# Two graph layers on one core: waits of a per-node stage as listed rounds, the first bias additions as a tied GpSimd step, and the last strip's square and copy on VectorE

## The chip, the cores and the metric

One core of a Trainium2 chip runs the whole program. A core has five engines with a queue each: TensorE (PE, matmuls; its weight loads are shown apart as PEld), VectorE (DVE), ScalarE (ACT), GpSimd (POOL) and SyncE (SP, which here only issues DMAs). An engine starts the instructions of its queue in order, so an instruction that waits holds up everything behind it on that engine. The metric is the device time of one execution in microseconds (us), the median of several runs; lower is better.

## The reference

Inputs are `x` of 3327 x 64 (fp32), and a symmetric 0/1 matrix `adj` of 3327 x 3327. Two graph layers follow each other, each with a layer norm and a ReLU ahead of it and a residual after it.

```
h  = relu(layernorm(x));     x = x + L0(h, adj)      # hyperbolic attention
h  = relu(layernorm(x));     out = x + L1(h, adj)    # decaying sum over neighbours
L0: adj_att[i,j] = sigmoid(left[i] + right[j] + b) * adj[i,j]
    support[i]   = sum_j adj_att[i,j] * logmap(h[i], h[j])        # N x N x 64
    L0 = proj(expmap(h, support))                                 # per node
L1: rank = cumsum(adj, axis=1); w[i,j] = adj[i,j] * 0.5^(neighbours of i at or behind j), at most 100 neighbours
    L1 = w @ (h @ weight) + bias
```

The sums over j in L0 and L1 are the heavy part; `expmap`, `proj`, the residual and the second layer norm are work per node, that is on 3327 x 64 numbers or less.

## The kernel before, in words

**Tiling.** Nodes are padded to 26 blocks of 128 (`NB`). The columns i are cut into four strips (`STRIPS`): blocks 0 to 7, 8 to 15, 16 to 21 and 22 to 25; they are called strips 0 to 3 here. Within a strip the loop at L1276 runs over rounds, one source block j at a time (two in strip 3, since it is half as wide). Strips 0, 1 and 2 have 26 rounds each and strip 3 has 13, so n counts rounds 0 to 90: 26 to 51 are strip 1, 52 to 77 strip 2, 78 to 90 strip 3.

**One round.** ScalarE computes the two `gelu` passes over the logmap's inner products (L881, on the PSUM tile `pq`), the sigmoid's tanh (L671) and sometimes the reading of the neighbour counts `pc` out of PSUM into bytes (`read`, L656). VectorE does `pair_one` (L676: tanh times adjacency, both operands in SBUF), often `read` (L658 or L660), `edges` (L622: the 0/1 mask of a later round) and `pair_two` (L681: times `pq`, which is in PSUM). TensorE does the counts (L633, L634), the inner products (L688, L689) and the sum over j (L701). The counts are what layer 1 later turns into its weights.

**Per-node stage.** When a strip's sum over j is ready, `strip_out` copies it out of PSUM (L1205, L1207), `turn` transposes it, and `post` (L1021) runs the per-node work: dot products, `expmap`, `proj`, residual, layer norm, and at last `s2`, the half-precision pair of rows that the matmuls of layer 1 take as weights. `post` is a Python generator that runs while the program is being written, and sets where its instructions stand between those of the rounds. For strips 0 to 2 (`hidden`) its small arithmetic is on GpSimd and it is spread over the rounds of the next strip. A `yield` of `BIG`, `LATER`, `ACT` or `POOL` hands the turn back: `advance` (L1236) takes portions up to a limit and stops at a `LATER`; a step that asks for `ACT` or `POOL` is emitted at the next place of a round where `asked_of` (L1246) allows it. In strips 0 to 2 each round calls `advance` once, and in strip 3 twice. `after(time)` (L1075) emits the GpSimd arithmetic asked for so far and then yields `LATER` so many times:

```
yield from [LATER] * math.ceil(time / ROUND[k + 1])
```

with `ROUND` a round's length per strip. The three waits are `after(7)` before the tanh (L1136), `after(16)` before the four wide GpSimd steps (L1172 to L1175), and `after(6)` before the normalized rows (L1193). This gives 2, 5, 2 rounds for strip 0, 3, 6, 3 for strip 1, and 4, 9, 4 half rounds for strip 2. What has not been emitted when the next strip's stage begins is emitted at once by `finish` (L1253). Such a stage keeps its tiles (`w`, `u`, `agg` and others) in single buffers, so the next strip's stage reuses them.

**A tie.** TensorE, VectorE and ScalarE keep the order in which the program is written. GpSimd's order is arranged by a planner from the data each instruction needs. A wide GpSimd step is therefore tied to a place: `on_pool` (L1085) first writes one element of the result out of the newest mask (L1089), which makes the step wait for that mask.

**The end.** After round 90 the bytes of 22 of the 26 source blocks are decoded into weights, either by one ScalarE instruction (L1376) or by two on VectorE (L1379, L1380), while TensorE runs through the blocks j of `order` (L1394), seven matmuls of L1269 each. Decoding runs `LEAD` blocks ahead of them. Of the 22 decodings the 3rd, 5th, 8th, 10th, 13th, 15th, 18th and 20th are on ScalarE. In the same loop the rest of strip 2's stage and all of strip 3's stage (not hidden: its arithmetic is on VectorE, powers apart) are advanced. The last four blocks, 22 to 25, need strip 3's `s2`; their matmuls (from L1438) come after that, interleaved with copying out of PSUM (L1417 to L1421), the matmul with `weight` (L1429), the last addition (L1431) and the stores (L1434, L1436). The layer's `bias` is added to the residual `x_sb` before that: blocks 0 to 15 by four GpSimd instructions written in the loop over `order` and tied to nothing, the rest by VectorE in the closing part (both L1392).

Of the kernel before, what the change touches and what calls it, by code (L numbers as in the profile page):

```python
# [12 lines left out]
F32 = mybir.dt.float32  # L13
# [5 lines left out]
AF = mybir.ActivationFunctionType  # L19
ALU = mybir.AluOpType  # L20
# [3 lines left out]
P = 128  # L24
N = 3327
NB = 26
NP = NB * P
D = 64
K = D + 2
STRIPS = [(0, 8), (8, 8), (16, 6), (22, 4)]  # L30
# [6 lines left out]


PORTIONS, LAST = (2, 4, 4, 8), 8
BIG, LATER, ACT, POOL = 4, 99, 100, 101  # L40
ROUND = (3.5, 3.5, 2.8, 1.9)

LEAD = 7
BESIDE, GAPS = (1, 2, 3, 4), (2, 4)
ACT_DECODES = (2, 5)

GSTRIPS = [(0, 7), (7, 7), (14, 6), (20, 6)]
GFMAX = 7 * P
# [400 lines left out]
def fast(ctx, tc, x, adj_t, r, w_att, b_att, weight, bias, out, flag):  # L449

    nc = tc.nc
    V, A, G, T = nc.vector, nc.scalar, nc.gpsimd, nc.tensor
    const = ctx.enter_context(tc.tile_pool(name="f_const", bufs=1))
# [7 lines left out]
    def across(src, n, name):  # L461
        t = const.tile([P, n], F32, name=name)
        nc.gpsimd.dma_start(t, bass.AP(tensor=src.tensor, offset=src.offset, ap=[[0, P], [1, n]]))
        return t
# [61 lines left out]
    def wide(t, n):  # L526
        return t[:, :, None].to_broadcast([P, n, D])
# [11 lines left out]
    s2 = const.tile([P, NB, 2, D], F16, name="s2")  # L539
# [122 lines left out]
    wide_step, last_on_act, last_mask = [False], [False], [None]  # L662
# [202 lines left out]
    for to, of in ((jz[:D], iz[D:]), (jz[D:], iz[:D]), (ju[:D], iu[:D]), (ju[D : D + 3], iu[D + 3 : D + 6]),  # L865
                   (ju[D + 3 : D + 6], iu[D : D + 3]), (ju[KB : KB + 7], iu[D:])):
        nc.gpsimd.dma_start(to[:, first_i], of)
    bias_b = across(bias, D, "bias_b")
    for half in (slice(0, D), slice(D, P)):
        nc.gpsimd.dma_start(w2[half], weight)  # L870

# [149 lines left out]
    def post(agg, k):  # L1021
# [5 lines left out]
        b0, nb = STRIPS[k]  # L1027
        bs = slice(b0, b0 + nb)
        hidden = k + 1 < len(STRIPS)
        asked_of_w = []  # L1030
        W = Asked(G if hidden else V, asked_of_w)

        def tile_of(name, *dims):
            return pool.tile([P, *dims], F32, name=name if hidden else name + "_last")

        def mul(y, a, b):
            W.tensor_mul(y, a, b)
# [32 lines left out]
        def do_asked():  # L1070
            for do, args, kwargs in asked_of_w:
                do(*args, **kwargs)
            asked_of_w.clear()

        def after(time):  # L1075

            for do, args, kwargs in asked_of_w:
                do(*args, **kwargs)
                if not hidden:
                    yield from [LATER] * 2 if kwargs.get("op") == ALU.pow else [1]  # L1080
            asked_of_w.clear()
            if hidden:
                yield from [LATER] * math.ceil(time / ROUND[k + 1])

        def on_pool(op, to, *of):  # L1085
            if hidden:
                yield POOL
                if last_mask[0] is not None:
                    G.tensor_copy(to[:, 0, :1], last_mask[0][:, :1])  # L1089
                getattr(G, op)(to, *of)  # L1090
                yield 0
            else:
                getattr(V, op)(to, *of)  # L1093
                yield BIG
# [4 lines left out]
        hs, v, xs = hw[:, bs, :D], agg[:, :, :D], x_sb[:, bs]  # L1099
# [3 lines left out]
        t0, t1, k_, y2, rn, rt = (tile_of(n, nb) for n in ("t0", "t1", "k", "y2", "rn", "rt"))  # L1103
        u, w = tile_of("u", nb, D), tile_of("w", nb, D)
# [26 lines left out]
        root(rn, t0)  # L1131
        mul(t0, t0, rn)
        mul(t0, t0, sk[:, bs])
        yield from after(7)
        yield ACT
        A.activation(k_, t0, AF.Tanh)  # L1136
        yield 0
# [30 lines left out]
        W.tensor_scalar(rn, rn, maxnorm, 1.0, op0=ALU.mult, op1=ALU.min)  # L1168
        mul(of_end, of_end, both(rn))
        mul(of_end[:, 0], of_end[:, 0], ih[:, bs])  # L1170
        yield from after(16)
        yield from on_pool("tensor_mul", w, hs, wide(of_end[:, 0], nb))  # L1172
        yield from on_pool("tensor_mul", u, v, wide(of_end[:, 1], nb))
        yield from on_pool("tensor_add", v, xs, w)
# [3 lines left out]

        V.tensor_reduce(t0, xs, AX.X, ALU.add)
        yield BIG  # L1180
        W.tensor_scalar(t0, t0, 1.0 / D, None, op0=ALU.mult)
        do_asked()
        yield from on_pool("tensor_sub", w, xs, wide(t0, nb))
        yield ACT
        A.activation(u, w, AF.Square)
        yield 0
        V.tensor_reduce(t0, u, AX.X, ALU.add)
        yield BIG
        W.tensor_scalar(t0, t0, 1.0 / D, EPS_LN, op0=ALU.mult, op1=ALU.add)
        root(rn, t0)  # L1190
        W.tensor_scalar(rn, rn, HS, None, op0=ALU.mult)
        yield from after(6)
        V.scalar_tensor_tensor(w, w, 0.0, wide(rn, nb), op0=ALU.max, op1=ALU.mult)  # L1193
        yield BIG
        yield ACT
        A.copy(s2[:, bs, 0], w)
        yield 0
        yield from on_pool("tensor_sub", s2[:, bs, 1], w, s2[:, bs, 0])

    def strip_out(k):  # L1200
# [58 lines left out]
    late = STRIPS[-1][0]  # L1259
# [16 lines left out]
    for n in range(2, R):  # L1276
        k, lo, hi = rounds[n]
        m, w = n + AHEAD, span(n)
# [84 lines left out]
    with tc.tile_pool(name="l1", bufs=2, reuse_waits="tile") as l1, tc.manual_schedule(engines=IN_ORDER):  # L1363
        decoded = 0

        def decode(j):

            nonlocal decoded
            if j in JD:
                return behind(j)  # L1370
            spare = decoded % (7 + len(JD)) - 7
            wt = weight_of[:, spare] if spare >= 0 else l1.tile([P, NP], U16, name="wt", bufs=7)
            decoded += 1
            to = by_parity(wt)
            if decoded * ACT_DECODES[0] % ACT_DECODES[1] < ACT_DECODES[0]:
                A.activation(to, behind(j).rearrange("p (k r) -> p r k", r=2), AF.Copy, scale=128.0)  # L1376
            else:
                pairs_of = behind(j).bitcast(U16)
                V.tensor_scalar(to[:, 0], pairs_of, 0xFF, 7, op0=ALU.bitwise_and, op1=ALU.logical_shift_left)  # L1379
                V.tensor_scalar(to[:, 1], pairs_of, 0xFF00, 1, op0=ALU.bitwise_and, op1=ALU.logical_shift_right)  # L1380
            return wt

        every = [*order, *range(late, NB)]
        weights = {j: decode(j) for j in every[: len(JD) + 1]}
        stages.append(Stage(per_node(len(STRIPS) - 1, pa)))
        pw[6] = ps.tile([P, FMAX], F32, name="pc")
        for n, j in beside:
            add(j, behind(j), n)

        def bias(b0, nb, engine=G):  # L1390
            xb = x_sb[:, b0 : b0 + nb]
            engine.tensor_add(xb, xb, bias_b[:, None, :].to_broadcast([P, nb, D]))  # L1392

        for i, j in enumerate(order):  # L1394
            for jn in every[: i + 1 + LEAD]:
                if jn not in weights:
                    weights[jn] = decode(jn)
            list(asked_of(ACT))
            list(asked_of(POOL))
            advance(LAST)  # L1400
            for n in range(len(chunks)):
                if j not in JD or n > 4:
                    add(j, weights[j], n)
            if i % 4 == 3 and i < STRIPS[-2][0]:
                bias(i - 3, 4)
        finish()
        for j in range(late, NB):
            if j not in weights:
                weights[j] = decode(j)
        kept_of = [l1.tile([P, min(NP - 1024 * q, 1024)], F32, name="ow" if q < 3 else "ow_last", bufs=2 if q < 3 else 1)  # L1410
                   for q in range(4)]

        def copied(n):
            q, r = chunks[n]
            to = kept_of[q].rearrange("p (k r) -> p r k", r=2)
            if r is None:
                V.tensor_copy(to, by_parity(pw[n][:, :256]))  # L1417
            elif r == 0:
                V.tensor_copy(to[:, 0], pw[n])
            else:  # L1420
                A.copy(to[:, 1], pw[n])  # L1421

        def close(q):
            for h in range(0, 8 if q < 3 else 2, 4):
                b0 = 8 * q + h
                nb = min(4, NB - b0)
                pc = pw[2 * q + h // 4]
                for b in range(nb):
                    T.matmul(pc[:, b * D : (b + 1) * D], kept_of[q][:, (h + b) * P : (h + b + 1) * P], w2s, start=True, stop=True)  # L1429
                o = l1.tile([P, 4, D], F32, name="o", bufs=4)  # L1430
                V.tensor_add(o[:, :nb], pc[:, : nb * D].rearrange("p (b d) -> p b d", d=D), x_sb[:, b0 : b0 + nb])  # L1431
                full = nb if b0 + nb < NB else nb - 1
                f0 = b0 * P
                nc.sync.dma_start(out[f0 : f0 + full * P, :].rearrange("(b p) d -> p b d", p=P), o[:, :full])  # L1434
                if full < nb:
                    nc.scalar.dma_start(out[f0 + full * P : N, :], o[: N - f0 - full * P, full])  # L1436

        for n in range(len(chunks)):  # L1438
            for j in range(late, NB):
                add(j, weights[j], n)  # L1440
            copied(n)
            if n == 2:
                bias(STRIPS[-2][0], late - STRIPS[-2][0], V)
                bias(late, NB - late, V)
            if n > 0 and n % 2 == 0:
                close(n // 2 - 1)
        close(3)
# [52 lines left out]
```

## Time and profile before

| | |
|---|---|
| median of 3 runs | 398.67 us (398.03 to 398.76) |
| the profiled execution, its own time | 398.52 us |
| its span, first to last instruction | 396.7 us |
| busy: DVE, PE, ACT, POOL | 364.2, 350.1, 348.5, 143.2 us |
| DVE, PE, ACT busy from 217 to 290 us (73 us, strip 2) | 71.89, 69.76, 71.84 us |
| DVE, PE, ACT busy from 345 to 377 us (32 us, decoding) | 29.39, 30.12, 22.56 us |
| from the last store's issue (389.2 us) to the end of the span | about 7.5 us |

The busy times say that no single engine is the limit over the whole span: three engines are each near nine tenths. Which of them ends last has to be read stretch by stretch. Rounds of strip 2 take about 2.7 us and of strip 3 about 3.7 us. In a line of the timeline the first number is the start, the second the duration, then engine, source line, operation and tiles; what stands in brackets is how long the engine sat idle before it, and what it waited for.

### The profile page before, as it was taken

To read this page: it belongs to the slowest core of one execution; us is meant where nothing else is said; L and a number is where in the kernel's file an instruction comes from. 1 tells how busy PE (TensorE), PEld (TensorE's weight loads), DVE (VectorE), ACT (ScalarE), POOL (GpSimd) and SP (SyncE) were. 2 spreads that over 40 slices of the span, in tenths; PEclk is the share of its full clock that TensorE was granted. 3 is DMA by queue.
4 is the path that set the end of the run, shared out by engine and by line. 5 is a ranking of instruction groups with operands and counts; after the bars stand their busy time and mean duration, and the time that the engine had idled before them with its cause. 6 is when DMAs were issued, how large, how long until landed. Compare 5 with 4: busy or idle time off the path is not lost.

```text
span 396.7 us, 4776 instructions
## 1 busy us (share of the span) xinstructions
PE 350.1 (88%) x1460; PEld 149.3 (38%) x1460; DVE 364.2 (92%) x551; ACT 348.5 (88%) x401; POOL 143.2 (36%) x279
## 2 busy tenths in 40 slices
PE   0067999999999899999998999999977899999892
PEld 0053333333333333333333354444433333344362
DVE  3999999999999999999999999999998999798941
ACT  2589999999999999999999999999988899697510
POOL 8136200000000166932133674851248678234100
PEclk9999999999999999999999999999999999999996
DMA  7314555455557455545445445555644430000022
GB/s 208 150 43 132 177 141 145 142 161 156 159 159 211 133 154 158 159 127 164 137 129 151 121 134 161 153 136 151 192 133 135 122 107 0 2 0 1 2 47 48
DMA packets 23299, 49.00 MB, mean 124 GB/s; under 512 B 8789, under 2 KB 9245, under 8 KB 23265
## 3 DMA queue, kind: packets, MB, share of 16 engines
q1 hardware_dynamic: 20993, 47.66, 41.2%
q10 hardware_dynamic: 1808, 0.46, 0.6%
q0 software_dynamic: 464, 0.49, 0.5%
q8 instruction: 13, 0.21, 0.2%
q14 instruction: 21, 0.17, 0.1%
HBM read 46.40 MB, written 0.87 MB: 119 GB/s over the span
## 4 chain that ended last, share of the span: by engine, by line
DVE 42%; ACT 25%; issue 15%; PE 13%; POOL 2%; DMA 1%; POOLq 0%; DVEq 0%; ACTq 0%
DVE sg L676 12%; DVE sg L681 12%; ACT pq L881 10%; ACT sg L671 7%; PE po L701 4%; DVE mask L622 3%; ACT behind_lo L656 2%; ACT behind_hi L656 2%; PE pc L633 1%; DMA x_sb<-in_x 1%; DVE behind_hi L660 1%; DVE behind_lo L660 1%; PE pc L634 1%; PE pq L688 1%; PE pq L689 1%
## 5 line engine op out<-in xcount | busy, mean ns | idle before, releaser
L881 ACT ACTIVATE pq<-pq 128x1024 f32<-128x1024 f32 (+1 forms) x182 | 173.7, 960 | 2.6 <-PE pq L689 0.8
L701 PE MATMUL po<-sg,hw 128*65 128x512 f32 (+1 forms) x364 | 159.7, 562 | 0.1
L681 DVE SCALAR_TENSOR_TENSOR sg<-pq,sg 128x1024 f32<-128x1024 f32 (+1 forms) x91 | 103.7, 1140 | 3.1 <-ACT pq L881 2.4
L676 DVE SCALAR_TENSOR_TENSOR sg<-sg,ad 128x1024 f32<-128x1024 f32 (+1 forms) x91 | 105.5, 1160 | 0.1
L671 ACT ACTIVATE sg<-left_b,right 128x1024 f32<-128x1024 f32 (+2 forms) x103 | 101.7, 987 | 0.0
L701 PEld LDWEIGHTS po<-sg,hw 128*65 128x65 f32 x364 | 48.9, 137 | 67.1 <-issue 52.8
L633 PE MATMUL pc<-mask,ca 128*128 128x512 bf16 (+1 forms) x175 | 63.5, 363 | 8.9 <-ACT behind_hi L656 3.5
L688 PE MATMUL pq<-iu,ju 71*128 71x512 f16 (+1 forms) x182 | 66.5, 366 | 1.1 <-ACT jz L818 0.8
L634 PE MATMUL pc<-mask,cb 128*128 128x512 bf16 (+1 forms) x182 | 64.7, 366 | 1.6 <-DVE mask L622 1.6
L689 PE MATMUL pq<-iz,jz 128*128 128x512 f16 (+1 forms) x182 | 65.0, 364 | 0.0
L622 DVE TENSOR_SCALAR mask<-ad 128x1024 bf16<-128x1024 f32 (+1 forms) x91 | 59.2, 652 | 0.0
L634 PEld LDWEIGHTS <-cb 128*128 128x128 bf16 x182 | 17.7, 97 | 47.5 <-issue 34.6
L1108 POOL CAST w<-mask 128x1 f32<-128x1 bf16 x3 | 1.5, 505 | 89.3 <-DVE mask L622 89.2
L633 PEld LDWEIGHTS <-ca 128*128 128x128 bf16 x175 | 17.1, 98 | 30.5 <-issue 18.3
L688 PEld LDWEIGHTS <-ju 71*128 71x128 f16 x182 | 17.8, 98 | 23.1 <-DVE sg L681 5.4
L1269 PEld LDWEIGHTS <-s 128*128 128x128 f16 x182 | 17.7, 98 | 21.3 <-DVE s L1093 2.3
L689 PEld LDWEIGHTS <-jz 128*128 128x128 f16 x182 | 17.9, 98 | 18.7 <-issue 1.1
L660 DVE TENSOR_SCALAR behind_lo<-pc 128x1024 uint8<-128x1024 f32 (+2 forms) x24 | 24.4, 1019 | 0.3 <-PE pc L634 0.3
L656 ACT ACTIVATE behind_hi<-pc 128x1024 uint8<-128x1024 f32 (+2 forms) x25 | 21.8, 873 | 1.6 <-PE pc L634 1.6
L656 ACT ACTIVATE behind_lo<-pc 128x1024 uint8<-128x1024 f32 (+2 forms) x24 | 20.8, 865 | 0.0
L852 PE MATMUL pq<-id,nui 128*71 128x128 f16 x8 | 1.0, 312 | 21.4 <-ACT nzi L826 21.4
L660 DVE TENSOR_SCALAR behind_hi<-pc 128x1024 uint8<-128x1024 f32 (+2 forms) x15 | 14.8, 985 | 0.9 <-PE pc L634 0.7
(344 smaller groups left out, 382.6 us busy)
## 6 DMA issues: line engine op xcount, KB each, us to landing
ad<-in_adj_t SPq DMA_DIRECT2D x65, 512.0 KB, 3.6
ad<-in_adj_t SPq DMA_DIRECT2D x26, 384.0 KB, 3.2
out<-o SPq DMA_DIRECT2D x6, 128.0 KB, 1.9
left_b<-left_d SPq DMA_DIRECT2D x1, 512.0 KB, 4.5
x_sb<-in_x ACTq DMA_DIRECT2D x1, 416.0 KB
x_sb<-in_x SPq DMA_DIRECT2D x1, 416.0 KB, 5.2
left_b<-left_d SPq DMA_DIRECT2D x1, 384.0 KB
jz<-iz POOLq DMA_DIRECT2D x2, 128.0 KB, 2.6
```

Source lines behind the costliest of these rows:

```text
L622: V.tensor_scalar(*args, 0.0, None, op0=ALU.not_equal)
L633: T.matmul(S.pc[:, f0:f1], ca, S.before[:, f0:f1], start=False, stop=True, skip_group_check=True)
L634: T.matmul(S.pc[:, f0:f1], cb, now[:, f0:f1], start=S.first, stop=True, skip_group_check=True)
L656: A.activation(kept, of, AF.Relu, scale=128.0 if j in JD else 1.0)
L660: V.tensor_scalar(kept, S.pc[:, : S.F], 0.0, None, op0=ALU.max)
L671: A.activation(part(n, sg, j), S.left[:, : S.F], AF.Tanh, bias=right[:, j : j + 1], scale=0.5)
L676: V.scalar_tensor_tensor(sg, sg, 1.0, ad_of.pop(n)[:, :w], op0=ALU.add, op1=ALU.mult)
L681: V.scalar_tensor_tensor(sg, pq_of.pop(n)[:, :w], WD, sg, op0=ALU.add, op1=ALU.mult)
L688: T.matmul(part(n, pq, j, f0, f1), ju[:KB, j, :], S.iu[:, f0:f1], start=True, stop=False)
L689: T.matmul(part(n, pq, j, f0, f1), jz[:, j, :], S.iz[:, f0:f1], start=False, stop=True)
L701: T.matmul(po[: D + 1, : f1 - f0], hw[:, j, :], part(n, sg_of[n], j, f0, f1), start=j == NB - 1, stop=j == 0)
L881: A.activation(pq, pq, AF.Gelu, scale=scale)
```

## The change

Five edits, all to where work stands or on which engine it is done; the sums over j are untouched.

1. The three waits of a hidden stage become a table by strip: 2, 5, 2 rounds for strip 0 (as before), 2, 5, 2 for strip 1 (one fewer each), 4, 10, 3 half rounds for strip 2 (one more, one fewer).
2. The biases of blocks 0 to 15 are added inside the stages of strips 0 and 1, by one GpSimd instruction per strip, as a step of its own ahead of the last wait. It is tied to the newest mask by an instruction that rewrites one column of `bias_b` with the mask times 0 plus a kept copy of that column, `bias_c`. The four untied additions go.
3. In the last strip, the mean's product and the subtraction are one VectorE instruction; the square and the half-precision copy go from ScalarE to VectorE, and are no longer steps that ask for ScalarE.
4. The eight decodings on ScalarE become the 2nd, 5th, 7th, 10th, 12th, 15th, 17th and 20th.
5. `LEAD` goes from 7 to 6.

```diff
+WAITS = ((2,5,2), (2,5,2), (4,10,3))
-LEAD = 7
+LEAD = 6
-ACT_DECODES = (2, 5)
+ACT_DECODES = (2,5,7,10,12,15,17,20)
...
     bias_b = across(bias, D, "bias_b")
+    bias_c = const.tile([P, 1], F32, name="bias_c")
+    G.tensor_copy(bias_c, bias_b[:, :1])
...
-                yield from [LATER] * math.ceil(time / ROUND[k + 1])
+                yield from [LATER] * WAITS[k][time]
...
-        yield from after(7)
+        yield from after(0)
...
-        yield from after(16)
+        yield from after(1)
...
-        W.tensor_scalar(t0, t0, 1.0 / D, None, op0=ALU.mult)
-        do_asked()
-        yield from on_pool("tensor_sub", w, xs, wide(t0, nb))
-        yield ACT
-        A.activation(u, w, AF.Square)
-        yield 0
+        if hidden:
+            W.tensor_scalar(t0, t0, 1.0 / D, None, op0=ALU.mult)
+            do_asked()
+            yield from on_pool("tensor_sub", w, xs, wide(t0, nb))
+        else:
+            V.scalar_tensor_tensor(w, wide(t0, nb), -1.0 / D, xs, op0=ALU.mult, op1=ALU.add)
+            yield BIG
+        if hidden:
+            yield ACT
+            A.activation(u, w, AF.Square)
+            yield 0
+        else:
+            V.tensor_mul(u, w, w)
+            yield BIG
...
-        yield from after(6)
+        if k + 2 < len(STRIPS):
+            do_asked()
+            yield POOL
+            G.tensor_scalar(bias_b[:, :1], last_mask[0][:, :1], 0.0, bias_c, op0=ALU.mult, op1=ALU.add)
+            G.tensor_add(xs, xs, bias_b[:, None, :].to_broadcast([P, nb, D]))
+            yield 0
+        yield from after(2)
...
-        yield ACT
-        A.copy(s2[:, bs, 0], w)
-        yield 0
+        if hidden:
+            yield ACT
+            A.copy(s2[:, bs, 0], w)
+            yield 0
+        else:
+            V.tensor_copy(s2[:, bs, 0], w)
+            yield BIG
...
-            if decoded * ACT_DECODES[0] % ACT_DECODES[1] < ACT_DECODES[0]:
+            if decoded in ACT_DECODES:
...
-            if i % 4 == 3 and i < STRIPS[-2][0]:
-                bias(i - 3, 4)
```

## The prediction

> **What bounds the kernel now.** I read the chain of waits first. Where it leaves the usual VectorE or ScalarE rounds for a GpSimd line, a per-node stage is on the path that sets the end (columns: start, duration, engine, tile, line).
>
> ```profile
> 301.42 1.13 DVE sg L681
> 303.95 1.82 POOL s L1090
> 306.44 1.01 POOL w L1109
> 308.49 1.13 DVE sg L681
> ...
> 363.36 1.31 POOL rn_last L1078
> 364.69 0.88 DVE rt_last L1078
> 376.88 1.04 PE po L1269 x4
> ```
>
> There are two places: the handover from strip 1's stage to strip 2's (round 80), and strip 3's own stage among the decodings. I then read the timelines of VectorE and GpSimd at the handover.
>
> ```profile
> 293.78 1.79 DVE L676 SCALAR_TENSOR_TENSOR sg<-sg,ad 128x1024 f32<-128x1024 f32 x1
> 297.29 0.67 DVE L1187 TENSOR_REDUCE t<-u 128x8 f32<-128x512 f32 x1
> 302.48 0.67 DVE L1193 SCALAR_TENSOR_TENSOR w<-w,rn 128x512 f32<-128x512 f32 x1
> 305.28 1.04 DVE L622 TENSOR_SCALAR mask<-ad 128x1024 bf16<-128x1024 f32 x1
> 307.48 0.55 DVE L1114 TENSOR_REDUCE dots<-w 128x6 f32<-128x384 f32 x1 [1.15 <-POOL w L1109]
> ```
>
> ```profile
> 293.76 2.39 POOL L1392 TENSOR_TENSOR x_sb<-x_sb,bias_b 128x256 f32<-128x256 f32 x2
> 303.95 1.82 POOL L1090 TENSOR_TENSOR s<-w,s 128x512 f16<-128x512 f32 x1 [0.75 <-ACT s L1196]
> 306.44 1.00 POOL L1109 TENSOR_TENSOR w<-hw,agg 128x384 f32<-128x384 f32 x1
> ```
>
> Strip 1's last rows (L1193) come so late that its last GpSimd step holds up strip 2's first one, for which VectorE idles 1.15. Also, the two untied biases start with an L676, which takes 1.79 where its neighbours take 1.2, and L622 takes 1.04 beside the late GpSimd step where 0.68 is usual. VectorE has no slack there (20.0 of 20 busy from 270 to 290), so each of these moves the rounds. Last, TensorE's timeline at the end.
>
> ```profile
> 374.73 0.27 PE L1269 MATMUL pc<-wt,s 128*128 128x256 bf16 x1
> 376.88 1.04 PE L1269 MATMUL po<-weight_of,s 128*128 128x512 bf16 x4 [1.88 <-DVE s L1093]
> ```
>
> From 346 to 375.0 TensorE has no gap (18 blocks of seven matmuls at 1.404 each from 349.56 on), then it waits 1.88 for strip 3's `s2`. So no reordering there gains more than 1.88: then TensorE is the limit.
>
> **What the Trainium skill says.** "SBUF — State Buffer", section "Who interferes with whom": a VectorE instruction with two SBUF inputs, or in a two-port mode, and a GpSimd instruction that reads SBUF exclude each other; whichever is first holds the other for its whole length. A VectorE instruction with one SBUF input outside these modes doesn't contend. The trace agrees: L676 (`sg` and `ad`, both SBUF) is the one stretched beside the biases, while L681 (`pq` in PSUM) at 292.63 keeps its 1.23 beside a GpSimd subtraction of 1.04. "VectorE: DVE Perf Modes", section "Mode 2×_2P", gives `tensor_scalar` from SBUF to SBUF two ports: that covers L622 and the decodings (L1379, L1380), and one of those took 1.22 instead of 0.58 at 353.06 beside a GpSimd subtraction.
>
> **Part 1, the waits.** I walked the yields by hand. Strip 0's steps keep their rounds up to the new bias step. Strip 1's tanh moves from round 61 to 60; its wide steps, both reductions and the square move two rounds earlier (second reduction: 79 to 77). Its normalized rows, with the new bias step in round 79, still fall in round 80, but now in that round's first `advance`, ahead of L681; before, `finish` put them behind it. Are the earlier steps ready? Tanh: its input was ready at 241.3, round 60's place is about 243.3: yes. First wide step: its factors came at 262.9, so 260.3 with the tanh a round (2.6) earlier; its tie comes two rounds before 266.5, at 261.2: yes, by 0.9. If not, it runs into an L676, at most 1. Strip 2's steps are the same chain of GpSimd work, limited by its data (of_end ready at 334.8, tied step begun at 334.8), so one half round more costs nothing.
>
> The handover then, step by step on VectorE: 0.6 more in round 77 (L1187 arrives), which takes the place of a 0.33 wait for ScalarE in round 78, so +0.2; no stretched L676 in round 79, −0.6; no L1187 there, −0.6. This is −1.0 at round 80. L1193 goes ahead of L681 and so ends at 300.95 instead of 303.1; ScalarE's copy (it idled 1.08 for it) and GpSimd's last step (0.9 to 1.3 without a rival) end by 303, strip 2's first step, behind an L676, by 304.9. VectorE reaches L1114 at about 304.9 to 305.5 instead of 307.48: the 1.15 wait is gone, the 0.36 of L622 perhaps not. Gain 2.0 to 2.6 if ScalarE and TensorE follow; ScalarE had 0.32 + 1.08 + 1.13 idle between 301 and 312, TensorE more. I take 1.9. Lower end 0: GpSimd's order is arranged by a planner and could still put the stages in each other's way.
>
> **Part 2, the tied bias.** Removed: four additions of 0.73 to 1.71 on GpSimd. Added: two of 128x512 (nearest row: the tied addition into `x_sb`, 1.19) and two small ones (0.2 to 0.3). They start behind a mask, beside L681, where nothing contends. The 0.57 gain is counted above; at strip 0's biases (213.77, 1.39 for 1.22) another 0.17, which I leave out. In round 53 it stands behind a root that ends at 222.6 and ahead of a step that waits for ScalarE until 225.9, so its 1.5 are hidden. The copy to `bias_c` takes 0.2 in GpSimd's 4.3 idle before 14.2, where it waits for `weight`. No DMA is moved.
>
> **Parts 3 to 5, the end.** VectorE's stream from 345.06 to 376.83 is 31.8 long. It has the same 14 decodings (1.0 each). Added: square and copy, 0.34 to 0.45 each (row L1112, 0.42); removed: the mean's product, 0.2. Removed waits: 0.27 (tanh) + 0.42 and 0.40 (powers). By sum: 31.8 + 0.8 − 0.2 − 1.1 = 31.3. Laying out the new order instruction by instruction, with starts 0.5 apart per half decoding, 0.34 or 0.45 per 256-wide step, 0.08 or 0.2 per small one and 1.1 for collisions with GpSimd, I get 30.8. So VectorE ends at 375.9 to 376.3 in the old clock instead of 376.8. But the order matters more: `s2` of strip 3 comes before the last two decodings (about 373.5), and the last decoding is needed only by the fourth matmul after 375.0, at 375.65. TensorE thus stops for 0.2 to 0.7 instead of 1.88: gain 1.2 to 1.6; I take 1.6. Bounds: 0 if VectorE ends as before, 1.88 if TensorE never stops. Cover for the smaller lead: by the layout each decoding is done over 2.5 before TensorE reaches it, and strip 2's `s2`, before ready 0.9 ahead of its first use, is 3 ahead. Without that cover TensorE would stop one for one. ScalarE's eight decodings (2.9 each) keep 23 of 31 us. Closing, 376.88 to the end, is unchanged at 19.8.
>
> **Sum.** The profiled execution took 398.52 (span 396.7, 1.82 around it): 398.52 − 1.9 − 1.6 = 395.0. The median is 0.15 above it: 395.2.
>
> **Rivals.**
> - *Only the end gains:* the handover's wait stays, since strip 2's first step still queues behind strip 1's last, or ScalarE is the limit there: its rounds in strip 3 sum to 3.58 (two `gelu` starts 0.94 apart, two tanh 0.61, a read 0.48) against VectorE's 3.47 (L676 and L681 1.13 each, L622 and a read 0.60 each). Against it: ScalarE idles in just these rounds. 398.7 − 1.6 = 397.1.
> - *Only the handover gains:* VectorE is the end's limit (29.4 of 32 busy) and the 0.8 added to it eats the removed waits; the last decoding, now behind `s2`, comes at the old time. 398.7 − 1.9 = 396.8.
> - *Slower:* in the end stretch strip 2's root (seven GpSimd instructions, 3.8 before) starts a block later and VectorE needs it 1.1 after it ends. Decodings use both ports, and the trace has a power of 2.72 instead of 1.35 and small steps of 1.1 instead of 0.2. Each microsecond of stretch over 1.1 stops VectorE, behind which the other decodings queue. It decides from 1.1 + 1.6 + 1.9 = 4.6 of stretch; at 6, 400.1. Against it: this root ran among decodings before, in 3.8.
> - *No change:* GpSimd's planner keeps the handover as it is and VectorE's stream ends as late: 398.6.
>
> **How the numbers follow.** Chances: both gains 0.50 (395.2, its own range 394.0 to 396.2), only the end 0.22, only the handover 0.14, no change 0.07, slower 0.07. A change under 0.2% (0.8 us) can't be told from none here. So faster 0.86, same 0.07, slower 0.07. The range 394.0 to 398.0 leaves out the slower case, most of the unchanged one, and a little below.
>
> **What would show it.** Right: no wait of L1114 for POOL in round 81, L1193 ahead of L681 in round 80, no L676 of 1.8 beside a bias, no L1392 on GpSimd; TensorE's wait before the first four L1269 of the last blocks under 0.8, and not on `s`. Wrong: L1114 still waiting; a wait of VectorE's `w` (L1193) or `rt` on POOL in the end stretch; gaps of TensorE between 346 and 375; L676 stretched beside the new bias step.

## The result, and the profile after

The changed kernel takes 396.23 us, the median of 8 runs (395.69 to 397.31); the kernel before, on the same chip, takes 399.12 (8 runs, 397.6 to 400.8). The ratio is 0.9937 with a 95% interval of 0.9916 to 0.9958: 2.9 us or 0.6% less, and the interval stays clear of 1. The profiled execution took 395.89, with a span of 394.1 (before: 398.52 and 396.7).

In some executions TensorE's clock dips early in the span and shifts everything behind it by 1 to 2 us (last section), so I compare stretches between marks that every trace has, not spans. Mark A is the start of strip 1's first product reduction (L1114 before, L1117 after; `dots<-w` 128x8, round 55), B the same of strip 2 (128x6, round 81), C VectorE's copy of strip 3's sum (65x512, after round 90), D its first copy of the closing part (`ow<-po`). A to B holds the handover, C to D is the end stretch.

| | A | B | C | D | A to B | C to D |
|---|---|---|---|---|---|---|
| before | 230.59 | 307.48 | 345.06 | 377.96 | 76.89 | 32.90 |
| after | 230.85 | 306.13 | 343.87 | 375.17 | 75.28 | 31.30 |

So the handover gave 1.61 and the end 1.60. B to C is 0.16 longer, A is 0.26 later, and from D to VectorE's last start it is 11.19 in both: 2.79 in all. From that last start to the end of the span it is 7.74 where it was 7.55, so that the spans differ by 2.6.

First VectorE's timeline at the handover in the changed kernel (start, duration, engine, line, operation, tiles, times).

```profile
290.17 0.67 DVE L1198 TENSOR_REDUCE t<-u 128x8 f32<-128x512 f32 x1
...
294.23 1.21 DVE L677 SCALAR_TENSOR_TENSOR sg<-sg,ad 128x1024 f32<-128x1024 f32 x1
...
300.62 0.68 DVE L1210 SCALAR_TENSOR_TENSOR w<-w,rn 128x512 f32<-128x512 f32 x1
301.23 1.21 DVE L682 SCALAR_TENSOR_TENSOR sg<-pq,sg 128x1024 f32<-128x1024 f32 x1
...
302.83 1.70 DVE L677 SCALAR_TENSOR_TENSOR sg<-sg,ad 128x1024 f32<-128x1024 f32 x1
...
305.06 1.15 DVE L623 TENSOR_SCALAR mask<-ad 128x1024 bf16<-128x1024 f32 x1
306.13 0.54 DVE L1117 TENSOR_REDUCE dots<-w 128x6 f32<-128x384 f32 x1
```

And GpSimd's timeline there.

```profile
296.79 0.27 POOL L1206 TENSOR_SCALAR bias_b<-mask,bias_c 128x1 f32<-128x1 bf16 x1
297.14 1.28 POOL L1207 TENSOR_TENSOR x_sb<-x_sb,bias_b 128x512 f32<-128x512 f32 x1
...
302.30 1.16 POOL L1093 TENSOR_TENSOR s<-w,s 128x512 f16<-128x512 f32 x1 [0.95 <-ACT s L1214]
303.52 1.06 POOL L1111 CAST w<-mask 128x1 f32<-128x1 bf16 x1
304.66 1.00 POOL L1112 TENSOR_TENSOR w<-hw,agg 128x384 f32<-128x384 f32 x1
```

Gone are the 1.15 for which VectorE waited ahead of the reduction (L1117 has no bracket) and the `pair_one` of 1.79 beside the biases (L677 at 294.23 takes 1.21). The new bias step stands beside L682, and nothing is stretched by it. Strip 1's rows (L1210) come ahead of L682. New is an L677 of 1.70: strip 1's last GpSimd step runs from 302.30 to 303.46, and an L677 whose work began then, at the usual 1.13 from one start to the next, would end at 304.59; the line ends at 304.53. Behind that L677 GpSimd's one-column cast takes 1.06 instead of 0.18, and the product behind it holds L623 (1.15, where 0.68 is usual) until 305.66. This chain is as the Trainium skill has it in "SBUF — State Buffer", section "Who interferes with whom": whoever comes first holds the other for its whole length.

TensorE's timeline at the end of the decoding.

```profile
373.53 0.27 PE L1290 MATMUL pc<-wt,s 128*128 128x256 bf16 x1
373.64 0.81 PE L1290 MATMUL po<-weight_of,s 128*128 128x512 bf16 x3
374.75 0.38 PE L1290 MATMUL po<-weight_of,s 128*128 128x512 bf16 x1 [0.30 <-DVE weight_of L1400]
```

The wait of 1.88 for `s` is gone. Three of the last blocks' matmuls start at once; the fourth waits for the last decoding, of which the bracket names the first half (L1400). Three starts of 0.215 from 373.64 end at 374.29, and the fourth starts at 374.75: a stop of 0.46, of which the bracket shows 0.30.

Why `s` is earlier shows in VectorE's timeline: it is done at 373.20 and two decodings (two instructions each) come after it; before, no decoding came after it. First the changed kernel, then the kernel before:

```profile
372.44 0.29 DVE L1217 CAST s<-w_last 128x256 f16<-128x256 f32 x1
372.77 0.43 DVE L1096 TENSOR_TENSOR s<-w_last,s 128x256 f16<-128x256 f32 x1
...
374.62 0.59 DVE L1401 TENSOR_SCALAR weight_of<-behind_hi 128x1664 uint16<-128x1664 uint16 x1
```

```profile
375.91 0.58 DVE L1380 TENSOR_SCALAR weight_of<-behind_hi 128x1664 uint16<-128x1664 uint16 x1
376.41 0.42 DVE L1093 TENSOR_TENSOR s<-w_last,s 128x256 f16<-128x256 f32 x1
```

Last the chain of waits (start, duration, engine, tile, line). GpSimd's lines at the handover are gone from it; the 1.62 of L677 is the new piece.

```profile
301.30 1.14 DVE sg L682
302.91 1.62 DVE sg L677
307.13 1.13 DVE sg L682
```

### The profile page after: what moved, and what is told of

Its sections match the earlier page's. It is cut to its first block, busy times and chain, and to the rows that moved or that the text cites. A ratio compares the mean times of both kernels' runs of the same rounds, so it can differ in the third digit from the quotient of the medians.

```text
span 394.1 us, 4754 instructions
## 1 busy us (share of the span) xinstructions
PE 350.7 (89%) x1436; PEld 151.5 (38%) x1460; DVE 364.5 (92%) x552; ACT 347.6 (88%) x399; POOL 144.7 (37%) x279
## 4 chain that ended last, share of the span: by engine, by line
DVE 43%; ACT 26%; issue 15%; PE 12%; DMA 1%; DVEq 0%; ACTq 0%
DVE sg L682 13%; DVE sg L677 13%; ACT pq L884 10%; ACT sg L672 8%; PE po L702 4%; DVE mask L623 3%; ACT behind_hi L657 2%; ACT behind_lo L657 2%; DMA x_sb<-in_x 1%; DVE behind_hi L661 1%; PE pc L635 1%; DVE behind_lo L661 1%; DVE wt L1400 1%; DVE wt L1401 1%; PE pq L690 1%
## 5 line engine op out<-in xcount | busy, mean ns | idle before, releaser
L682 DVE SCALAR_TENSOR_TENSOR sg<-pq,sg 128x1024 f32<-128x1024 f32 (+1 forms) x91 | 103.5, 1138 | 2.7 <-ACT pq L884 1.8
L677 DVE SCALAR_TENSOR_TENSOR sg<-sg,ad 128x1024 f32<-128x1024 f32 (+1 forms) x91 | 105.2, 1156 | 0.1
L634 PE MATMUL pc<-mask,ca 128*128 128x512 bf16 (+1 forms) x170 | 61.9, 364 | 7.2 <-DVE behind_hi L661 2.8
L635 PE MATMUL pc<-mask,cb 128*128 128x512 bf16 (+1 forms) x168 | 59.7, 365 | 1.6 <-DVE behind_lo L661 1.3
L623 DVE TENSOR_SCALAR mask<-ad 128x1024 bf16<-128x1024 f32 (+1 forms) x91 | 59.2, 651 | 0.0
```

The lines of the kernel that those rows point to most:

```text
L623: V.tensor_scalar(*args, 0.0, None, op0=ALU.not_equal)
L634: T.matmul(S.pc[:, f0:f1], ca, S.before[:, f0:f1], start=False, stop=True, skip_group_check=True)
L635: T.matmul(S.pc[:, f0:f1], cb, now[:, f0:f1], start=S.first, stop=True, skip_group_check=True)
L677: V.scalar_tensor_tensor(sg, sg, 1.0, ad_of.pop(n)[:, :w], op0=ALU.add, op1=ALU.mult)
L682: V.scalar_tensor_tensor(sg, pq_of.pop(n)[:, :w], WD, sg, op0=ALU.add, op1=ALU.mult)
```

## The experiments

Theory 1 is the prediction's: the waits free the handover by taking strip 1's late rows and the two biases out of it, and square, copy and decodings free the end. Its rivals were that one part does all of it, or that the waits and the end are tied to each other. Below, each run has its median and its ratio to the kernel before on the same chip, and A to B and C to D are from its profile. Two profiles of the changed kernel differ by 0.18 in A to B (75.28, 75.46) and by 0.03 in C to D (31.30, 31.27). In the kernel before, A to B can be 0.5 shorter with nothing changed in it; the run e4 below shows why.

### The waits alone, and the bias alone

**e1_waits**: the kernel before, with the table of waits and nothing else.

```diff
+WAITS = ((2,5,2), (2,5,2), (4,10,3))
-                yield from [LATER] * math.ceil(time / ROUND[k + 1])
+                yield from [LATER] * WAITS[k][time]
```

> The kernel before with the table of waits alone (2, 5, 2 / 2, 5, 2 / 4, 10, 3); biases untied in the end loop, end as before. Theory (handover and end gain apart, and the handover's gain is that strip 1's last rows come before strip 2's first GpSimd step is due): L1193 moves to round 79, the L1114 of round 81 waits less than 0.3 for GpSimd, the two untied biases now run in round 77 and stretch that round's L676 by about 0.5; in all 1.3 to 2.0 us less than before, TensorE's wait of 1.9 for s at the end stays. Rival 'only the end gains': within 0.3 of before. Rival 'the tie of the bias made the handover's gain': within 0.3 of before, with L1114 still waiting about 1.1.

**e2_bias**: the kernel before, with the tied bias step in place of the four untied additions.

```diff
+        if k + 2 < len(STRIPS):
+            do_asked()
+            yield POOL
+            G.tensor_scalar(bias_b[:, :1], last_mask[0][:, :1], 0.0, bias_c, op0=ALU.mult, op1=ALU.add)
+            G.tensor_add(xs, xs, bias_b[:, None, :].to_broadcast([P, nb, D]))
+            yield 0
...
-            if i % 4 == 3 and i < STRIPS[-2][0]:
-                bias(i - 3, 4)
```

> The kernel before with the tied bias step alone (old waits 3, 6, 3 for strip 1). Theory: the step falls into round 80, between strip 1's root and its last step, so GpSimd's queue at the handover is 1.5 longer; no L676 stretched in round 79 (0.57 less), but L1114's wait of 1.15 grows to 1.5 to 2.5: between 0.3 less and 1.0 more than before. Rival 'the tie of the bias made the handover's gain': 0.6 to 1.3 less than before.

Measured: e1 396.70, ratio 0.9948 (0.9929 to 0.9967), A to B 75.26, C to D 32.43. e2 399.89, ratio 1.0035 (1.0021 to 1.0049), A to B 77.32, C to D 32.93. VectorE's timeline at the handover, first e1, then e2:

```profile
303.56 1.21 DVE L677 SCALAR_TENSOR_TENSOR sg<-sg,ad 128x1024 f32<-128x1024 f32 x1
...
305.30 0.89 DVE L623 TENSOR_SCALAR mask<-ad 128x1024 bf16<-128x1024 f32 x1
306.11 0.54 DVE L1115 TENSOR_REDUCE dots<-w 128x6 f32<-128x384 f32 x1
```

```profile
302.23 1.62 DVE L1201 SCALAR_TENSOR_TENSOR w<-w,rn 128x512 f32<-128x512 f32 x1
...
308.18 0.55 DVE L1116 TENSOR_REDUCE dots<-w 128x6 f32<-128x384 f32 x1 [1.16 <-POOL w L1111]
```

And GpSimd's timeline of e2, where the tied step of 1.26 stands beside L1201:

```profile
302.03 1.26 POOL L1198 TENSOR_TENSOR x_sb<-x_sb,bias_b 128x512 f32<-128x512 f32 x1
```

The waits alone give the whole handover (75.26 against 75.28 with all edits). One expectation of e1 failed: TensorE's wait for strip 3's `s` did not stay at 1.88 but is 1.41. The reason comes under strip 2's waits.

The tied bias alone is slower, by 0.43 in A to B: no `pair_one` is stretched beside it in round 79, but with the old waits its step falls beside strip 1's rows, which come late already, and holds them (1.62 for 0.67). The wait for GpSimd was expected to grow to 1.5 or more, and stays at 1.16. The median is 1.4 higher, more than was expected and more than A to B explains; in the profile another 0.87 lies behind VectorE's last start (8.42 to the end of the span, 7.55 before), and its cause stays open. That moving the biases is good or bad depends on where the waits put it.

### The end alone, and its halves

**e3_end**: the kernel before, with edits 3, 4 and 5 of the change. **e4_square**: with edit 3 only. **e5_decodings**: with edits 4 and 5 only.

```diff
# e3 = e4 + e5; e4:
-        yield ACT
-        A.activation(u, w, AF.Square)
-        yield 0
+        if hidden: ...
+        else:
+            V.tensor_mul(u, w, w)
+            yield BIG
...
# e5:
-LEAD = 7
+LEAD = 6
-ACT_DECODES = (2, 5)
+ACT_DECODES = (2,5,7,10,12,15,17,20)
```

> The kernel before with the three edits of the end alone (square and copy on VectorE, the listed decodings, lead 6). Theory: strip 3's s ends ahead of the last two decodings, TensorE stops at most 0.8 before the last blocks instead of 1.88: 1.2 to 1.8 us less than before, the handover as before (L1114 waits about 1.1). Rival 'VectorE's added 0.8 eats the removed waits': within 0.4 of before.

> The kernel before with the square and the copy on VectorE alone (lead 7, decodings as before). Theory (the order counts, not the hops to ScalarE): s still comes behind the 22nd decoding, VectorE's stream is as long as before within 0.5, TensorE waits 1.2 to 1.9 for s: 0 to 0.6 us less than before. Rival 'the hops to ScalarE were the loss': 1.2 to 1.8 less, as with all three edits.

> The kernel before with the listed decodings and lead 6 alone (square and copy still on ScalarE). Theory (square and decodings pay only together, since only then does s come ahead of the last two decodings): s still comes behind the 22nd decoding, TensorE waits 1.2 to 1.9 for it, the end stretch (from the copy of strip 3's sums to the first copy of a result) is 32.3 to 33.0 long as before's 32.9. Rival 'the order of the decodings is the whole gain': the end stretch is 31.3 to 31.8, TensorE waits under 0.8.

| | median | ratio | A to B | C to D | TensorE's last wait for `s` |
|---|---|---|---|---|---|
| before | 398.5 | 1 | 76.89 | 32.90 | 1.88 |
| e4_square | 400.10 | 1.0033 (1.0017 to 1.0049) | 76.37 | 33.50 | 2.48 |
| e5_decodings | 397.66 | 0.9980 (0.9969 to 0.9992) | 76.90 | 32.14 | 1.12 |
| e3_end | 397.09 | 0.9953 (0.9936 to 0.9970) | 76.89 | 31.72 | 0.70 |

TensorE's timeline, the first matmuls that need strip 3's `s`, in e4 and in e3:

```profile
378.61 1.04 PE L1281 MATMUL po<-weight_of,s 128*128 128x512 bf16 x4 [2.48 <-DVE s L1093]
```

```profile
376.83 1.04 PE L1281 MATMUL po<-weight_of,s 128*128 128x512 bf16 x4 [0.70 <-DVE s L1093]
```

e4 was a miss: alone, the moved square and copy make the end longer. In its trace VectorE still waits for the tanh and for both roots' powers (0.27, 0.43 and 0.40, as in the kernel before), and has the added work on top. In e5 and e3 only the last of these waits is left. e5 alone gains 0.76 in C to D (its 32.14 and its wait of 1.12 lie between what its theory and its rival expected) and e4 loses 0.60, which would make a gain of 0.16; e3, with both, gains 1.18. So the decodings pay alone, and the square and the copy only beside them.

The order on VectorE shows why. The last decoding and `s`, first in e5, then in e3:

```profile
376.75 0.58 DVE L1380 TENSOR_SCALAR weight_of<-behind_hi 128x1664 uint16<-128x1664 uint16 x1
377.25 0.41 DVE L1093 TENSOR_TENSOR s<-w_last,s 128x256 f16<-128x256 f32 x1
```

```profile
376.35 0.43 DVE L1093 TENSOR_TENSOR s<-w_last,s 128x256 f16<-128x256 f32 x1
...
377.19 0.59 DVE L1392 TENSOR_SCALAR weight_of<-behind_hi 128x1664 uint16<-128x1664 uint16 x1
```

In e5 `s` still stands behind the last decoding; in e3 it stands ahead of it. Square and copy put 0.6 more into VectorE's stream ahead of `s` (e4), and the decoding that goes behind `s` takes 1.0 out: from C, `s` is done after 31.00 in e5 and after 30.59 in e3. In e4 the order is the old one, so only the 0.6 is left. ScalarE's decodings are not what held the two steps in e5: there ScalarE had stood idle for 1.20 ahead of the square and for 0.86 ahead of the copy.

e4 shows one thing more. From A to B it emits the same work as the kernel before, e3 and e5 (76.89, 76.89, 76.90), and has 76.37. The two untied additions and the `pair_one` of round 79 are the difference, in VectorE's and GpSimd's timelines of e4:

```profile
295.41 1.22 DVE L676 SCALAR_TENSOR_TENSOR sg<-sg,ad 128x1024 f32<-128x1024 f32 x1
```

```profile
295.40 3.02 POOL L1404 TENSOR_TENSOR x_sb<-x_sb,bias_b 128x256 f32<-128x256 f32 x2
```

In the kernel before, the two engines also start within 0.02 of each other, but there L676 takes 1.79 and the additions 2.39. So the same two steps, begun at nearly the same moment, can fall out either way, and about 0.5 of the handover's 1.61 is not there in every execution of the kernel before. The median of e4 (1.6 above before) fits neither stretch: its profile has the early dip of the clock, with A 1.64 later than before. So C to D, not the ratio, is what judges this edit.

Yet e3 leaves 0.70 of the wait, and one decoding behind `s`, not two. The changed kernel has 31.30, so 0.42 of the end comes from something that e3 lacks.

### What else is in the end: strip 2's waits

**e7_strip2_waits**: the changed kernel with strip 2's old number of half rounds.

```diff
-WAITS = ((2,5,2), (2,5,2), (4,10,3))
+WAITS = ((2,5,2), (2,5,2), (4,9,4))
```

> The changed kernel with strip 2's old waits 4, 9, 4. Theory (found in the run with the end's edits alone: strip 2's reduction a block later leaves its share of a block's portions to strip 3's stage, whose steps then come a block earlier): strip 3's s comes 1.0 to 1.5 later, TensorE waits 0.6 to 0.8 for s and the end stretch is 31.6 to 31.9 long instead of 31.3, so 0.3 to 0.6 more than the changed kernel. Rival (the prediction's word, 'costs nothing'): within 0.15 of it.

Measured: 396.38, ratio 0.9944 (0.9926 to 0.9963), A to B 75.41, C to D 31.70. TensorE's timeline:

```profile
375.61 1.04 PE L1290 MATMUL po<-weight_of,s 128*128 128x512 bf16 x4 [0.69 <-DVE s L1096]
```

The wait for `s` is back at 0.69, as in e3 (0.70), and e1, which has strip 2's new waits but not the rest of the end, has 0.47 less than before. So strip 2's extra half round is worth 0.4 to 0.5 in the end stretch. The order of VectorE's instructions says how. In the two lines that follow, of e7 and then of the changed kernel, `t_last` is the last step ahead of strip 3's first root.

```profile
350.51 0.55 DVE L1182 TENSOR_REDUCE t<-x_sb 128x6 f32<-128x384 f32 x1
...
353.51 0.17 DVE L1081 TENSOR_SCALAR t_last<-d_last 128x4 f32<-128x4 f32 x1
```

```profile
350.51 0.17 DVE L1081 TENSOR_SCALAR t_last<-d_last 128x4 f32<-128x4 f32 x1
...
351.60 0.54 DVE L1182 TENSOR_REDUCE t<-x_sb 128x6 f32<-128x384 f32 x1
```

With one half round more, strip 2's reduction (L1182) comes after strip 3's first small steps and not among them. From C, `t_last` is at 6.64 in the changed kernel, and at 8.53 in e7 (before: 9.53; e1: 7.52). The portions of a round that strip 2's reduction no longer takes go to strip 3's stage, and its steps come one decoding earlier.

The half round has a price too. B to C is 37.58 in e7 and 37.74 in the changed kernel; it is 37.58 or 37.59 in all six profiles with strip 2's old waits, and 37.73 to 37.75 in all eight with the new ones. So the half round gains 0.40 and costs 0.16. The medians of e7 and of the changed kernel can't be told apart, which fits so small a net gain; this verdict rests on the traces. By the marks the parts add up: e1 gives 1.63 and 0.47, e3 gives 1.18 in the end, 3.28 together, and the changed kernel has 3.21.

### The tie of the bias

**e6_untied**: the changed kernel without the instruction that makes the bias wait for a mask.

```diff
-            G.tensor_scalar(bias_b[:, :1], last_mask[0][:, :1], 0.0, bias_c, op0=ALU.mult, op1=ALU.add)
```

> The changed kernel without the tie: the bias additions stand at the same place in the program, but nothing ties them to a mask. Theory (the tie keeps a wide GpSimd step off the VectorE instruction with two SBUF inputs): the planner runs the addition of strip 1 straight behind the subtraction in round 76, a round's L677 is stretched by 0.3 to 0.6, and the handover comes that much later than in the changed kernel: 0.3 to 0.7 more than it. Rival 'the place in the program is enough': within 0.2 of the changed kernel, no stretched L677 before round 81.

Measured: 396.88, ratio 0.9958 (0.9947 to 0.9970), A to B 76.28, C to D 31.25. VectorE's and then GpSimd's timeline of e6:

```profile
286.69 1.89 DVE L677 SCALAR_TENSOR_TENSOR sg<-sg,ad 128x768 f32<-128x768 f32 x1
```

```profile
286.50 1.27 POOL L1206 TENSOR_TENSOR x_sb<-x_sb,bias_b 128x512 f32<-128x512 f32 x1
```

Without the tie the planner places the addition as soon as its data are there, at 286.50 instead of 297.14, beside an L677, which takes 1.89 for 0.94. The cost in this profile, 1.00 in A to B, is above the 0.3 to 0.7 that I had expected: VectorE has no slack, and the 0.95 by which one instruction is stretched is paid in full.

### The rest of the handover and of the end

**e8_22nd**: one more decoding on ScalarE. **e9_last_wait**: strip 1's last wait taken out, so that its rows come a round earlier. **e10_both**: both. **e11_product**: e10, with strip 2's first product on VectorE instead of GpSimd.

```diff
# e8
-ACT_DECODES = (2,5,7,10,12,15,17,20)
+ACT_DECODES = (2,5,7,10,12,15,17,20,22)
# e9
-WAITS = ((2,5,2), (2,5,2), (4,10,3))
+WAITS = ((2,5,2), (2,5,0), (4,10,3))
# e11, beside e10's
-        if hidden:
+        if hidden and k != 2:
             G.tensor_copy(w[:, 0, :1], last_mask[0][:, :1])
             G.tensor_mul(w, hs, v)
             yield LATER
         else:
+            if hidden:
+                yield LATER
             V.tensor_mul(w, hs, v)
```

> The changed kernel with the 22nd decoding on ScalarE too, which idles there. Theory (VectorE's last decoding is all that still stops TensorE in the end): the stop of 0.45 before the fourth matmul of the last blocks goes, the end stretch is 30.8 to 30.9 long, 0.4 to 0.5 less than the changed kernel. Rival (ScalarE's decoding comes too late or something else is late at the same time): within 0.15 of it.

> The changed kernel with strip 1's last wait 0 rounds instead of 2. Theory (at the handover GpSimd's last step of strip 1 and first step of strip 2 still collide with VectorE's L677 and L623, 0.5 each, because the rows of L1210 come only in round 80): L1210 moves to round 79, the last step of strip 1 ends about 1 earlier, strip 2's first step starts as soon as its input is there, and L1117 of round 81 comes 0.5 to 1.0 earlier than in the changed kernel. Rival (the collision is set by when strip 2's sums are copied out, not by L1210): L1117 within 0.2, one of L677 and L623 still stretched.

> The changed kernel with the last wait 0 for strip 1 and the 22nd decoding on ScalarE. Theory (handover and end add up): the end stretch 30.8 to 30.9 long, and the time less than the changed kernel's by 0.45 plus what the last wait alone gives (0.5 to 1.0). Rival (the last wait gives nothing): 0.4 to 0.5 less, as with the decoding alone.

> As the run with both, and strip 2's first wide product is computed by VectorE in round 81 instead of GpSimd. Theory (what is left at the handover is GpSimd holding VectorE's two-input instructions): L677 and L623 of round 81 keep their 1.2 and 0.7, VectorE's stream is 0.45 longer by the product; 0.0 to 0.5 less than the run with both. Rival (ScalarE is the limit at the handover by now): within 0.2 of it although the collisions are gone.

**e12_changed** is the changed kernel once more, beside e10 and e11 on the same chip.

> The changed kernel once more, beside the three runs above on the same chip. Both readings: 2.0 to 3.0 less than before, 31.3 for the end stretch.

| | median | ratio | A to B | C to D |
|---|---|---|---|---|
| after (first runs) | 396.23 | 0.9937 (0.9916 to 0.9958) | 75.28 | 31.30 |
| e12_changed | 396.06 | 0.9939 (0.9920 to 0.9958) | 75.46 | 31.27 |
| e8_22nd | 395.52 | 0.9921 (0.9899 to 0.9944) | 75.42 | 30.85 |
| e9_last_wait | 395.72 | 0.9928 (0.9900 to 0.9956) | 75.16 | 31.27 |
| e10_both | 395.39 | 0.9919 (0.9889 to 0.9950) | 75.17 | 30.85 |
| e11_product | 395.77 | 0.9931 (0.9913 to 0.9949) | 75.53 | 30.84 |

e8: TensorE no longer stops, and VectorE is done early enough; C to D falls by 0.45 to TensorE's own length. TensorE's timeline of e8:

```profile
375.35 0.27 PE L1290 MATMUL pc<-wt,s 128*128 128x256 bf16 x1
375.46 1.03 PE L1290 MATMUL po<-weight_of,s 128*128 128x512 bf16 x4
```

e9 showed the theory behind it wrong, which took strip 1's late last step for the whole cause of the 0.96 still lost in L677 and L623. The step did move, and L677 took its 1.21 again, but A to B is only 0.12 shorter. VectorE's and GpSimd's timelines of e9:

```profile
298.78 1.51 DVE L677 SCALAR_TENSOR_TENSOR sg<-sg,ad 128x1024 f32<-128x1024 f32 x1
...
302.82 0.56 DVE L1248 COPY agg<-po 128x390 f32<-128x390 f32 x1 [0.20 <-PE po L1238]
303.31 1.21 DVE L677 SCALAR_TENSOR_TENSOR sg<-sg,ad 128x1024 f32<-128x1024 f32 x1
...
305.04 0.89 DVE L623 TENSOR_SCALAR mask<-ad 128x1024 bf16<-128x1024 f32 x1
```

```profile
303.53 1.84 POOL L1112 TENSOR_TENSOR w<-hw,agg 128x384 f32<-128x384 f32 x1 [0.30 <-DVE agg L1248]
```

Now strip 2's product waits only for the copying out of strip 2's own sums (L1248), and that waits 0.20 for TensorE to turn them. It starts a little behind L677, is held by it (1.84 for 1.00), and holds L623 in turn; and the bias step (297.94, 1.27) now meets an L677 (1.51). The rival's signs came: when strip 2's sums come out decides this collision. But the run is no clean test of what the late step costs. L677 and L623 gave back 0.49 and 0.26, while the L677 beside the bias step lost 0.30 and VectorE idled 0.20 for TensorE. In e11 the product leaves GpSimd, and L677 and L623 take 1.22 and 0.69, but the product's 0.55 then stands in VectorE's queue: no gain. VectorE's only wait there, from 299 to 312, is 0.19 for TensorE, so ScalarE, the rival, is not seen to be the limit.

e10 is the fastest version that ran, but its interval and the changed kernel's overlap: 0.17% between the medians beside e12 is not a difference that these runs can show. The 0.45 in C to D is seen in e8, e10 and e11 alike.

## Why the prediction was right, point by point

The forecast was 395.2 (range 394.0 to 398.0), with both gains the likeliest case: 1.9 at the handover and 1.6 at the end. Both came: 1.61 and 1.60 between the marks, and 396.23 by the median. On the ratio, 0.9937 of the 398.67 shown is 396.2, so the forecast took 0.9% off where 0.6% came, at the upper edge of this case's own range (394.0 to 396.2). The sum of the two gains, 3.5, met 3.21; the rest of the difference is 0.26 at A, 0.16 from B to C and 0.19 behind the last start, which nothing in the sum stood for.

- **Part 1, up to round 80: right.** The forecast was −1.0 by then. VectorE reaches the same place (L681 at 301.34 before, L1210 at 300.62 now) 70.75 after A before, and 69.77 after it now: −0.98. L1198 stands in round 77, no L677 is stretched in round 79, and L1210 stands ahead of L682 as walked through by hand. The 0.6 in it for the stretched L676 is partly luck: in e4 that instruction is not stretched in the old kernel either.
- **Part 1, from there to L1114: mis-sized.** The step that failed is "ScalarE's copy and GpSimd's last step end by 303". On ScalarE the copy stood behind a `read` and began at 301.54; GpSimd's step ended at 303.46. That overlap of 0.46 was not a mere delay: L677 started inside it and lost 0.49, GpSimd's one-column cast was then behind L677, strip 2's product ended at 305.66 instead of 304.9, and L623 lost 0.47, where it had lost 0.36 before. So −1.15 (the wait) + 0.49 + 0.11 is −0.55; measured is −0.63, and the forecast was −1.0 to −1.6. I had followed how late GpSimd would be, but not whom its step would hold up. That the total still came near 1.9 owes to a margin: 1.9 is below the 2.0 to 2.6 of the walk, and the prediction gives no term for the difference.
- **Part 2: right in its place and its duration, but its gain doesn't show.** The tied step takes 0.27 + 1.28 and stands beside L682; without the tie it costs 1.00 (e6). The forecast credited 0.57 to the biases leaving an L676. e1 keeps the old biases, and one of its L677 does take 1.34 for 0.94, yet its A to B is 75.26 and the changed kernel's 75.28. The reason is in e1's rows: they stand at 297.61, in round 79. The bias step is one more step ahead of them and puts them into round 80, next to strip 2's first step. The prediction had them in round 80, and did not ask where they would be without the bias step. What the stretched L677 cost in e1, its earlier rows gave back.
- **Strip 2's waits: wrong.** "One half round more costs nothing" missed that it gains 0.40 in the end, and costs 0.16 ahead of it (e7). It was judged on strip 2's own data, when what counted was whose portions of VectorE's queue it leaves free.
- **Parts 3 to 5: right in sum, with a wrong share.** By the sum, VectorE's stream was to be 31.3 long, by the layout 30.8; from C (343.87) to the end of the last decoding (375.21) it is 31.34. `s` before the last two decodings was right, and so were a stop of 0.2 to 0.7 (0.46) and the gain (1.60). But `s` is done 29.33 after C, not 28.4 (373.5 in the old clock), and the two decodings behind it come only with strip 2's extra half round: with edits 3 to 5 alone it is one, a stop of 0.70 and a gain of 1.18 (e3). So the 1.6 was met in part by luck: about 0.4 of it comes from a term that the prediction put at nothing.
- **The smaller lead: right.** TensorE has no wait between 346 and 373.6, so a lead of 6 is enough. The closing part was right too: from D on nothing changed (11.19).
- **The rivals.** *Only the end*, *only the handover* and *no change* are excluded by the marks: both gains were there. *Slower* did not come: strip 2's root runs among the decodings from 355.16 to 358.31, 3.15 long where 3.8 was the old length, and the longest power among them takes 1.46, so nothing near the 4.6 of stretch from which it would have decided.

What stays open: by which chain strip 2's extra half round makes B to C 0.16 longer, and why e2's median is higher than its stretches explain. That a version with strip 2's sums turned earlier would win the rest of the handover (0.96 of stretched L677 and L623) was not tried, nor one that has the rows early, as in e9, and keeps the bias step off an L677.

## What to carry to other kernels

Where an engine has no slack, look not only at how late a helper's step comes but at which instruction of the busy engine it will stand beside: a step of 0.5 too late stretched two instructions by 0.5 each here, since it held one, which then held the helper's next. Where two engines start such steps at nearly the same moment, look at more than one profile: the collision can fall out either way. Test parts of a bundled change alone: a tied addition and a square moved to another engine each made their own stretch longer alone (by 0.43 and by 0.60), and pay only beside the waits or the decodings that make room for them. And when a stage is delayed on purpose, ask who gets the turns that it gives up: that was worth 0.4 us.

## What the runs showed of the hardware that I had not expected

In five of the fourteen profiles (e3, e4, e5, e7, e8) TensorE's granted clock falls early, between 36 and 44 us: from 40 to 44 us it is 0.70 in e3, 0.61 in e4, 0.63 in e5, 0.67 in e7 and 0.59 in e8, and 1.00 in the other nine. TensorE's timeline of e3 and of the kernel before, at the same matmuls:

```profile
40.19 0.63 PE L688 MATMUL pq<-iu,ju 71*128 71x512 f16 x1
40.62 0.63 PE L689 MATMUL pq<-iz,jz 128*128 128x512 f16 x1
```

```profile
40.18 0.38 PE L688 MATMUL pq<-iu,ju 71*128 71x512 f16 x1
40.40 0.38 PE L689 MATMUL pq<-iz,jz 128*128 128x512 f16 x1
```

Matmuls of 512 columns start 0.43 apart instead of 0.22. Mark A is then at 231.7 to 232.5 instead of 230.1 to 230.9, so that two spans can differ by 1 to 2 us with nothing changed behind it. In e9 and e12 the clock falls a little sooner (0.57 and 0.65 from 32 to 36 us), and A is not late (230.69 and 230.14). e1 and e3, of which one shows it and the other doesn't, emit the same work up to there, so I take it for a property of the execution and not of an edit; what starts it was not looked into.

The second was the size of the mutual stops. A GpSimd cast of one column, 0.18 alone, took 1.06 behind an L677, and an addition of 128x512 of 1.27 made a VectorE instruction of 0.94 last 1.89. And in four profiles with the same work the same meeting of two instructions went three times against VectorE (1.79) and once against GpSimd (1.22 for VectorE, 3.02 for 2.39 on GpSimd).
